# Self attention, element by element: each phase dequantises its own weights, and the search takes three steps a unit

## The chip, the cores and the metric

The kernel runs on one core of a Trainium2 chip. The metric is device time in microseconds (us) of one execution, the median of several runs. A profile is one further execution, recorded by the hardware profiler; its span runs from the first to the last instruction. A core has TensorE (PE) for matmuls with its weight loads (PEld), VectorE (DVE), ScalarE (ACT), GpSimd (POOL) and SyncE (SP), which here issues nearly all DMA transfers. Each engine takes its instructions in the order of the built program; semaphores make one engine wait for another.

## What is computed

One decoder layer over two batch elements of 512 tokens and 512 features, in float32: self attention, cross attention and a feed-forward part, each added to its input and normalised.

```python
q, k, v = (x @ (codes * repeat(scales, 32)) + b  for wq, wk, wv)   # 16 heads of 128
attn = softmax(q @ k.T / sqrt(128))
x = layernorm(x + (attn @ v) @ (wo_codes * repeat(wo_scales, 32)) + bo)
s = coef * (x @ Wq.T) @ ctx.T              # 1024 context rows
s = where(s < 54th largest of the row, -inf, s)
x = layernorm(x + softmax(s) @ ctx @ Wo.T)
x = layernorm(x + (silu(x @ Wg.T) * (x @ Wu.T)) @ Wd.T)
```

The weights of self attention come as codes and scales: a weight is a code times the scale of its block of 32 rows. This multiplication is called dequantising; it must be done on the chip before a weight is used.

## The kernel before

**Units, groups and phases.** The work of one head of one element is a unit. Four heads make a group; a group of one element is a phase of four units. There are 16 heads, so four groups and, for two elements, eight phases and 32 units. The list `phases` (L648) sets their order: group 0 of element 0, group 0 of element 1, then groups 1 to 3 of element 0, then groups 1 to 3 of element 1. `half_way` (L650) is the number of the first unit after element 0's last: 20. Phase 1 has no weights of its own: `owner` (L653) sends it to those of phase 0.

**A phase.** `values` (L719) computes v of four heads. For each unit, `queries_keys` (L736) computes q and k, `weights` (L771) the scores (PE, L785), the softmax (DVE and ACT) and its transpose: DVE turns blocks of 32 by 32 into the tile tq (L810), and 16 DMAs a unit move them into the tile pt (L818). `attend` (L824) multiplies pt with v (PE, L830) into the tile ot. When a phase is over, `project` (L859) multiplies its ot by wo and adds the result to the residual: DVE adds one part (L875) and POOL the other (L877), but for group 3, where DVE adds both (L874, L875).

**Strassen's products.** Most matmuls go through `seven` (L187 for the matmuls, L197 for the copies out of PSUM): a block product in seven instead of eight matmuls, in Winograd's form. It needs four sums of blocks of each operand. For the weights POOL makes them: tile wc for q and k (L107 to L110, four operations of 128x256), vc for v and oc for wo (four of 128x512 each). For ot, POOL makes otc (L116 to L119). Of the seven products, PE runs numbers 1, 2, 5, 6, 7 and 4, and 3 last; product 1 needs the first half of the dequantised weights, 2 and 4 the second, and 5, 6, 7 and 3 need sums.

**Weights.** Per unit, one DMA brings the codes wqk (0.5 MB) and one the scales sqk (0.5 MB). Per phase, wv and wo come with 1 MB of codes and two times 0.5 MB of scales (sv, so). POOL dequantises (L684) in halves: two operations of 128x512 a unit, and four each for wv and wo. The scales pass through three buffers (sc0 to sc2, L675) in turn, so a load of scales waits until the third one before it has been used. wv has one tile, and so has wo: a load waits until PE has read the last phase's.

**Order.** The loop (L961 on) runs over i, the unit that is attended to, with u = i + 2 the unit whose q, k and weights are computed. `due` tells at which u the scales are dequantised: those of unit u at u - 1, those of wv three and two units before a phase, those of wo three and four units after its start. The loads of scales are traced one unit earlier. A scheduler then reorders the instructions of each engine; the order on SP and POOL is fixed when the program is built.

**Start.** The first two units' weights and the first wv are dequantised on DVE, those of units 2 and 3 on POOL (L922 on). x transposed of element 1 (`load_xT(1)`) is loaded at the start and combined by POOL (`combine_x`) at i = 0. `load_residual` (at i = 0) brings x and adds the bias on POOL, in eight operations of 128x512.

**Cross attention of element 0** begins when element 0's self attention is over, amid the units of element 1. At i = half_way comes the layer norm, then its transpose, at half_way + 3 the queries (PE, L380), and at half_way + 3, 4, 5 and 7 the four score blocks (PE, L474). `clip` (L483) searches each block's 54th largest value on DVE, in steps of one MATCH_REPLACE8 (L493) and one MAX8 (L496); four blocks have 28 steps. `step` (L956) takes two before and two after the transposes of each unit from i = half_way + 4 on, and what is left is done at the last unit but one.

Of the kernel before, what the change touches and what calls it, by code (L numbers as in the profile page):

```python
# [24 lines left out]
def decoder_layer(  # L25
# [21 lines left out]
    nc = tc.nc  # L47
    B, S, D = x.shape
# [8 lines left out]
    GH = 4  # L57
    GW = GH * P
    NG = H // GH
# [173 lines left out]
    def load_xT(b):  # L233

        xt = place(f"xT{b}", (KD, S), f"x0T{b}")
        for n in range(2):
            nc.sync.dma_start(
                out=xt[:, n * HK : (n + 1) * HK, :],
                in_=xT[b, n * HD : (n + 1) * HD, :].rearrange("(k p) s -> p k s", p=P),
            )  # L240
        xts[b] = xt

    def combine_x(eng, b, name):
        xcs[b] = combine_b(eng, blocks(xts[b]), place(f"xc{b}", (4, HK, HS), f"{name}c{b}"))

    def load_residual():

        bo_sb = place("mt0", (D,), "bo_sb")
        nc.sync.dma_start(out=bo_sb, in_=bo.to_broadcast([P, D]))
        for b in range(B):  # L250
            rb[b] = place(f"res{b}", (NT, D), f"res{b}")
            nc.sync.dma_start(out=rb[b], in_=x[b].rearrange("(t p) d -> p t d", p=P))
            for t in range(NT):
                res[b, t] = rb[b][:, t, :]
                nc.gpsimd.tensor_tensor(res[b, t], res[b, t], bo_sb, ALU.add)
# [389 lines left out]

    phases = [(0, 0), (0, 1)] + [(g, b) for b in range(B) for g in range(1, NG)]  # L648
    units = [(g, b, j) for g, b in phases for j in range(GH)]
    half_way = (NG + 1) * GH  # L650
    last = len(phases) - 1

    def owner(p):  # L653
        return 0 if p == 1 else p

    def place_of_qk(u):

        return (u if u < GH else (u - GH) % 5) if u < half_way else (1, 2, 0)[(u - half_way) % 3]

    qkw, vw, ow, ks, qs, pts, vs, ots, raw = {}, {}, {}, {}, {}, {}, {}, {}, {}  # L660
    parts = {}
# [9 lines left out]
    def load_scales(key, n, queue):  # L671
        w, scales = raw[key]
        at, sv = scales[n]
        part = w if at is None else w[:, at, :]
        sct = place(f"sc{scale_count[0] % 3}", tuple(part.shape[1:]), f"s{key}_{n}")  # L675
        scale_count[0] += 1
        queue.dma_start(out=sct, in_=sv)
        parts[key, n] = (part, part, sct)

    def dequantise(eng, key, n=0):  # L680
        part, codes, sct = parts.pop((key, n))
        k = part.shape[1] // 2
        for w in (slice(0, k), slice(k, None)) if eng is nc.gpsimd else (slice(None),):
            eng.tensor_tensor(part[:, w], codes[:, w], sct[:, w], ALU.mult)  # L684

    def load_qk(u):
        g, b, j = units[u]
        h = g * GH + j
        load(f"qk{u}", f"wqk{place_of_qk(u)}", (KD, 2, P), wqk[h], [(None, wqk_s[h])])
# [11 lines left out]
    def load_o(p):  # L701
        g, b = phases[p]
        load(
            f"o{p}",
            "v0" if p == last else "wo",
            (GH, D),
            wo[g * GW : (g + 1) * GW, :].rearrange("(k p) f -> p k f", p=P),
            [(slice(n * 2, (n + 1) * 2), wo_s[g, n]) for n in range(2)],
        )

    def combine_qk(eng, u):
        w = raw[f"qk{owner(u // GH) * GH + u % GH}"][0]
        qkw[u] = combine_a(eng, blocks_pair(w), place(f"wc{u % 2}", (4, HK, P), f"wc{u}"))

    def combine_v(eng, p):
        w = raw[f"v{owner(p)}"][0]
        vw[p] = combine_a(eng, blocks_t(w), place("cmb0", (4, HK, GW // 2), f"vc{p}"))

    def values(p):  # L719
# [135 lines left out]
    def combine_o(eng, p):  # L855
        w = raw[f"o{p}"][0]
        ow[p] = combine_a(eng, blocks_t(w), place("wv" if p == last else "cmb1", (4, GH // 2, HD), f"oc{p}"))

    def project(p):  # L859

        g, b = phases[p]
        lo, hi = ots.pop((p, 0)), ots.pop((p, 1))
        oc = combine_b(
            nc.vector if p == last else nc.gpsimd,
            (lo[:, :, :HS], lo[:, :, HS:], hi[:, :, :HS], hi[:, :, HS:]),
            place("cmb0", (4, GH // 2, HS), f"otc{p}"),
        )
        rr = rb[b].rearrange("p (h s) (c f) -> p h s c f", h=2, c=2)
        for s in range(NT // 2):

            def add(z, u, s=s, c=1):
                o = rr[:, :, s, c, :]
                if g == NG - 1:
                    nc.vector.tensor_add(o, o, u)  # L874
                nc.vector.tensor_add(o, z, o)  # L875
                if g < NG - 1:
                    nc.gpsimd.tensor_tensor(o, o, u, ALU.add)  # L877

            seven(
                f"o{p}_{s}",  # L880
                oc,
                ow[owner(p)],
                slice(s * P, (s + 1) * P),
                add,
                lambda z, u, add=add: add(z, u, c=0),
            )
        close()
# [19 lines left out]
    for n in range(2):  # L907
        f = first[1][n]
# [21 lines left out]
    load_scales("qk2", 0, nc.sync)  # L930
    load_qk(3)
    load_scales("qk3", 0, nc.sync)
    load_xT(1)
    dequantise(nc.gpsimd, "qk2")
    combine_qk(nc.gpsimd, 2)
    dequantise(nc.gpsimd, "qk3")
    load_o(0)
    load_scales("o0", 0, nc.sync)
    load_scales("o0", 1, nc.sync)
    dequantise(nc.gpsimd, "o0", 0)  # L940
    dequantise(nc.gpsimd, "o0", 1)
    combine_o(nc.gpsimd, 0)


    due = {}
    for p in range(2, len(phases)):
        for j in range(GH):
            due.setdefault(p * GH + j - 1, []).append((f"qk{p * GH + j}", 0))
        for n in range(2):
            due.setdefault(p * GH - 3 + n, []).append((f"v{p}", n))  # L950
            due.setdefault((p * GH + 3 if p < last else p * GH + 2) + n, []).append((f"o{p}", n))

    XS = [half_way + n for n in (3, 4, 5, 7)]
    search0 = clips(0, ("work",))
# [1 line left out]
    def step(n):  # L956
        for _ in range(n):
            next(search0, None)

    lag = 2  # L960
    for i in range(len(units)):  # L961
        g, b, j = units[i]
        u = i + lag
        if u < len(units):
            gu, bu, ju = units[u]
            if ju == 0:
                values(u // GH)
            queries_keys(u)
            for key, n in due.get(u, []):
                dequantise(nc.gpsimd, key, n)  # L970
                if key == f"qk{u + 1}":
                    combine_qk(nc.gpsimd, u + 1)
                    if ju == GH - 1:
                        combine_v(nc.gpsimd, (u + 1) // GH)
                if key[0] == "o" and n == 1:
                    combine_o(nc.gpsimd, int(key[1:]))
            if u + 1 < 2 * GH:
                combine_qk(nc.gpsimd, u + 1)
                if u + 1 == GH:
                    combine_v(nc.gpsimd, 1)  # L980
        p = i // GH
        if j == 0 and 0 < p < last:
            project(p - 1)
            if p > 1:
                load_o(p)
        if i == len(units) - 2:
            project(last - 1)
            load_xw("wo", xwo, "wo")
        attend(i)
        if i > half_way + 3:  # L990
            step(2)
        if u < len(units):
            weights(u)
            if i == last * GH - 1:
                load_o(last)
            if 2 * GH <= u + 3 < len(units):
                load_qk(u + 3)
            if ju == 0 and 1 < u // GH + 1 < len(phases):
                load_v(u // GH + 1)
            for key, n in due.get(u + 1, []):  # L1000
                load_scales(key, n, nc.sync)
        if i == 0:
            load_residual()
            combine_x(nc.gpsimd, 1, "x0")
        if i == 2 * GH:
            load_memT(0)
        if i == half_way:
            load_xw("wq", xwq, "cmb1")
            normal = normalise(0, "a")
            next(normal)  # L1010
        if i == half_way + 1:
            for _ in normal:
                pass
            turn_x(0, "xc0", "xT0", "x1T")
        if i == half_way + 3:
            xquery(0)
            score_tiles(0, (("wqk3", 1), ("wqk4", 1), ("xT0", 2)))
        if i in XS:
            xscores(0, XS.index(i))
        if i == XS[-1] + 1:  # L1020
            load_mem(0)
        if i > half_way + 3:
            step(2)
        if i == len(units) - 2:
            for _ in search0:
                pass
            free_sc = [f"sc{(scale_count[0] + n) % 3}" for n in range(3)]
            for _ in combine_mem(0, ("wqk2", *free_sc[:2])):
                pass
            transpose_weights(0, ("xT1", "xc1"))  # L1030
# [279 lines left out]
```

## Time and profile before

| | us |
|---|---|
| median of 3 runs | 1083.48 (1083.36 to 1083.54) |
| span of the profiled execution | 1082.2 |
| median less span | 1.3 |
| PE / PEld busy | 1070.7 / 796.8 |
| DVE / ACT / POOL busy | 611.0 / 408.6 / 575.6 |
| POOL: wqk dequantised (L684, 52 operations) | 66.2, 1.289 each |
| DMA moved | 142.71 MB |

A row of a timeline gives start, length, engine, line, operation, output tile and inputs, shape and count, and in brackets the idle time ahead of it and what ended that. A matmul of float32 appears as two records. A busy time is that of one engine; "idle before" is the time in which the engine did nothing ahead of such instructions. A stretch's row gives its length and the busy time and number of instructions of each engine, the granted TensorE clock, the share of the DMA engines and the GB/s.

### The profile page before, as it was taken

The page shows a single profiled execution, that of the slowest core. Times are in us where ns is not written, and L with a number is a line of the kernel's source. Part 1 is how long each engine was busy: PE and PEld are TensorE (multiplying, and loading weights), DVE is VectorE, ACT ScalarE, POOL GpSimd, SP SyncE. Part 2 cuts the span into 40 slices and gives each one's busy share as a digit, 9 for nine tenths or more (in the row PEclk, how much of TensorE's full clock was granted, in tenths as well). Part 3 has the DMA queues.
Part 4 walks back from the last instruction along what each step waited for, and adds up shares of the span by engine and source line. Part 5 has one row for each costly group of instructions (what it writes and reads, how often), then busy time and mean ns, then how long its engine had stood idle before and what let it go on. Part 6 is the DMA issues. An engine that isn't in the chain of part 4 may idle for free.

```text
span 1082.2 us, 12794 instructions
## 1 busy us (share of the span) xinstructions
PE 1070.7 (99%) x4252; PEld 796.8 (74%) x4252; DVE 611.0 (56%) x1015; ACT 408.6 (38%) x882; POOL 575.6 (53%) x578
## 2 busy tenths in 40 slices
PE   9999999999999999999999999999999999999997
PEld 5676776677677677665666567778888888888886
DVE  5444345335434445643898774468999736554254
ACT  3444435335344533733444353222443214221221
POOL 4955546846945856514952654525565812264530
PEclk9999999999999999999999999999999999999999
DMA  9535446545553555536332537331214401422201
GB/s 350 156 105 176 157 134 220 181 142 161 198 191 95 173 172 156 194 81 182 136 117 78 139 115 253 89 106 39 97 65 132 137 20 51 163 86 76 94 19 39
DMA packets 66257, 142.71 MB, mean 132 GB/s; under 512 B 12560, under 2 KB 12560, under 8 KB 66192
## 3 DMA queue, kind: packets, MB, share of 16 engines
q1 hardware_dynamic: 65472, 140.32, 41.4%
q10 hardware_dynamic: 720, 1.57, 0.4%
q8 instruction: 34, 0.56, 0.2%
q14 instruction: 31, 0.25, 0.1%
HBM read 99.90 MB, written 2.10 MB: 94 GB/s over the span
## 4 chain that ended last, share of the span: by engine, by line
PE 82%; DVE 13%; ACT 3%; DMA 1%; POOL 1%; issue 1%; DVEq 0%; ACTq 0%; POOLq 0%
PE sc L785 10%; PE av L830 9%; PE zqk L187 9%; PE zgu L187 7%; PE rqk L187 7%; PE rgu L187 5%; PE zo L187 5%; PE zv L187 5%; PE zpd L187 4%; PE ro L187 4%; DVE work L493 4%; DVE top L496 3%; PE rv L187 3%; PE rpd L187 3%; PE zxav L187 3%; PE xs L474 2%
## 5 line engine op out<-in xcount | busy, mean ns | idle before, releaser
L830 PE MATMUL av<-pt,v 128*128 128x512 f32 x256 | 121.8, 592 | 0.0
L796 DVE TENSOR_REDUCE nm<-sc 128x2 f32<-128x1024 f32 x63 | 76.9, 1222 | 78.9 <-PE sc L785 78.9
L785 PE MATMUL sc<-k,q 128*128 128x512 f32 x256 | 117.2, 599 | 0.0
L799 ACT ACTIVATE p<-sc,nm 128x512 f32<-128x512 f32 x128 | 86.8, 681 | 75.8 <-DVE nm L796 75.8
L810 DVE STREAM_TRANSPOSE tq<-p 128x512 f32<-128x512 f32 x128 | 84.9, 699 | 38.0 <-ACT p L807 36.2
L785 PEld LDWEIGHTS sc<-k,q 128*128 128x128 f32 x256 | 47.2, 190 | 62.4 <-issue 50.6
L807 ACT ACTIVATE p<-p,sm 128x512 f32<-128x512 f32 x128 | 85.4, 715 | 1.5 <-DVE sm L806 1.3
L107 POOL TENSOR_TENSOR wc<-wgu 128x256 f32<-128x256 f32 x32 | 24.9, 779 | 111.9 <-PE zgu L187 69.3
L684 POOL TENSOR_TENSOR wqk<-wqk,sqk 128x512 f32<-128x512 f32 x52 | 66.2, 1289 | 32.5 <-DMA wqk<-in_wqk 22.4
L197 ACT ACTIVATE ugu<-rgu 128x256 f32<-128x256 f32 x96 | 36.2, 378 | 103.0 <-PE rgu L187 100.8
L830 PEld LDWEIGHTS av<-pt,v 128*128 128x128 f32 x256 | 48.6, 190 | 30.5 <-issue 26.8
L187 PE MATMUL rgu<-x2c,wc 128*128 128x256 f32 x256 | 66.2, 381 | 1.0 <-ACT ugu L197 1.0
L187 PE MATMUL rqk<-x0c,wc 128*128 128x256 f32 x248 | 65.0, 384 | 0.3 <-ACT uqk L197 0.2
L496 DVE MAX8 top<-work 128x8 f32<-128x1024 f32 x48 | 58.6, 1221 | 0.9
L848 ACT ACTIVATE ot<-av,bqkv_sb 128x512 f32<-128x512 f32 x28 | 19.2, 687 | 101.4 <-PE av L830 101.4
L187 PEld LDWEIGHTS rgu<-x2c,wc 128*128 128x128 f32 x256 | 48.2, 190 | 8.9 <-ACT ugu L197 1.9
L187 PEld LDWEIGHTS rqk<-x0c,wc 128*128 128x128 f32 x248 | 45.1, 189 | 12.2 <-ACT uqk L197 5.1
L1134 DVE TENSOR_TENSOR gt<-zgu,ugu 128x512 f32<-128x512 f32 x32 | 21.9, 684 | 48.9 <-PE zgu L187 48.9
L107 POOL TENSOR_TENSOR wc<-wqk 128x256 f32<-128x256 f32 x31 | 22.6, 730 | 49.8 <-PE zqk L187 49.7
L493 DVE MATCH_REPLACE8 work<-top,work 128x1024 f32<-128x1024 f32 x40 | 48.3, 1208 | 0.0
L877 POOL TENSOR_TENSOR res<-res,uo 128x512 f32<-128x512 f32 x24 | 30.7, 1280 | 29.8 <-DVE res L875 26.2
L116 POOL TENSOR_TENSOR otc<-ot 128x512 f32<-128x512 f32 x7 | 8.9, 1270 | 66.9 <-PE zv L187 66.9
(313 smaller groups left out, 2465.8 us busy)
## 6 DMA issues: line engine op xcount, KB each, us to landing
pt<-tq SPq DMA_DIRECT2D x512, 64.0 KB, 2.0
wgu<-in_wgu SPq DMA_DIRECT2D x32, 512.0 KB, 3.2
wqk<-in_wqk SPq DMA_DIRECT2D x26, 512.0 KB, 5.5
sqk<-in_wqk_s SPq DMA_DIRECT2D x26, 512.0 KB, 4.1
wdn<-in_wdn SPq DMA_DIRECT2D x8, 1024.0 KB, 5.7
sv<-in_wv_s SPq DMA_DIRECT2D x14, 512.0 KB, 5.8
wv<-in_wv SPq DMA_DIRECT2D x7, 1024.0 KB, 5.2
wo<-in_wo SPq DMA_DIRECT2D x7, 1024.0 KB, 5.6
```

The source lines that it names most:

```text
L107: eng.tensor_tensor(c[0], a10, a11, ALU.add)
L187: nc.tensor.matmul(o, left[k][:, cols], right[k], start=start and k == 0, stop=k == len(left) - 1, skip_group_check=not start,)
L197: nc.scalar.activation(u[:, i, :], r, AF.Identity, bias=at, scale=scale)
L493: nc.vector.match_replace(work, top, src, LOWEST)
L496: nc.vector.max(top, work)
L684: eng.tensor_tensor(part[:, w], codes[:, w], sct[:, w], ALU.mult)
L785: nc.tensor.matmul(pair[n], q[:, (t + n) * P : (t + n + 1) * P], k, start=True, stop=True,)
L796: nc.vector.reduce_max(nms, scs, axis=AX.X, negate=True)
L799: nc.scalar.activation(pr, pair[t % 2], AF.Exp, bias=nms[:, t % 2 : t % 2 + 1], accum_out=sm,)
L807: nc.scalar.activation(pr, pr, AF.Copy, scale=sm)
L810: nc.vector.transpose(tq[:, :, :, t, :].rearrange("p n k c -> p k n c"), pr.rearrange("p (k n a) -> p k n a", n=NB, a=BLK),)
L830: nc.tensor.matmul(av, vs[u // GH][:, k, j * P : (j + 1) * P], pt[:, :, k, :], start=(k == 0), stop=(k == NT - 1),)
```

## The change

The phases run element by element: groups 0 to 3 of element 0, then groups 1, 2, 3 and 0 of element 1. `half_way` is 16. `owner` is gone: each phase loads, dequantises and combines its own weights, so phase 1 does so too. The entries of `due` are made for all phases, with the scales of phase 1's wv at u = 2 at the earliest. Element 1's x is loaded and combined at i = 10. wo of phase 0 is dequantised through `due` and not ahead of the loop. Of the search, one step is taken before and two after each unit's transposes. The last projection is now that of group 0, so POOL makes its second addition.

```diff
-    phases = [(0, 0), (0, 1)] + [(g, b) for b in range(B) for g in range(1, NG)]
+    phases = [(g, 0) for g in range(NG)] + [((g + 1) % NG, 1) for g in range(NG)]
     units = [(g, b, j) for g, b in phases for j in range(GH)]
-    half_way = (NG + 1) * GH
+    half_way = NG * GH
...
-    def owner(p):
-        return 0 if p == 1 else p
...
-        return (u if u < GH else (u - GH) % 5) if u < half_way else (1, 2, 0)[(u - half_way) % 3]
+        return u % 5 if u < half_way else (1, 2, 0)[(u - half_way) % 3]
...
-        w = raw[f"qk{owner(u // GH) * GH + u % GH}"][0]
+        w = raw[f"qk{u}"][0]
...
-        w = raw[f"v{owner(p)}"][0]
+        w = raw[f"v{p}"][0]
...
-                ow[owner(p)],
+                ow[p],
...
-    load_xT(1)
     dequantise(nc.gpsimd, "qk2")
     combine_qk(nc.gpsimd, 2)
     dequantise(nc.gpsimd, "qk3")
+    load_v(1)
     load_o(0)
-    load_scales("o0", 0, nc.sync)
-    load_scales("o0", 1, nc.sync)
-    dequantise(nc.gpsimd, "o0", 0)
-    dequantise(nc.gpsimd, "o0", 1)
-    combine_o(nc.gpsimd, 0)
+    load_qk(GH)
...
     due = {}
-    for p in range(2, len(phases)):
-        for j in range(GH):
+    for p in range(len(phases)):
+        for n in range(2):
+            if p:
+                due.setdefault(max(p * GH - 3 + n, 2), []).append((f"v{p}", n))
+            due.setdefault((p * GH + 3 if p < last else p * GH + 2) + n, []).append((f"o{p}", n))
+        for j in range(GH if p else 0):
             due.setdefault(p * GH + j - 1, []).append((f"qk{p * GH + j}", 0))
-        for n in range(2):
-            due.setdefault(p * GH - 3 + n, []).append((f"v{p}", n))
-            due.setdefault((p * GH + 3 if p < last else p * GH + 2) + n, []).append((f"o{p}", n))
+    for key, n in due[2]:
+        load_scales(key, n, nc.sync)
...
-            if u + 1 < 2 * GH:
+            if u + 1 < GH:
                 combine_qk(nc.gpsimd, u + 1)
-                if u + 1 == GH:
-                    combine_v(nc.gpsimd, 1)
...
             project(p - 1)
-            if p > 1:
-                load_o(p)
+            load_o(p)
...
         if i > half_way + 3:
-            step(2)
+            step(1)
...
-            if 2 * GH <= u + 3 < len(units):
+            if GH < u + 3 < len(units):
                 load_qk(u + 3)
-            if ju == 0 and 1 < u // GH + 1 < len(phases):
+            if ju == 0 and u // GH + 1 < len(phases):
                 load_v(u // GH + 1)
...
         if i == 0:
             load_residual()
+        if i == half_way - 6:
+            load_xT(1)
             combine_x(nc.gpsimd, 1, "x0")
```

## The prediction, made before the changed kernel had run

> **What bounds the kernel now.** I read the page first, its busy times.
>
> ```profile
> PE 1070.7 (99%) x4252; PEld 796.8 (74%) x4252; DVE 611.0 (56%) x1015; ACT 408.6 (38%) x882; POOL 575.6 (53%) x578
> ...
> PEclk9999999999999999999999999999999999999999
> ```
>
> TensorE (PE) is the bound: 1070.7 of 1082.2 us, at full clock. The two programs, listed engine by engine, hold the same instructions on PE, DVE and ACT (2144, 961 and 761 rows' worth); POOL gets 20 more and SP 14 more DMAs. So the change can only move PE's idle time, and that needs a view by stretches: us, PE busy, PEld, DVE, ACT, POOL, clock, DMA share, GB/s.
>
> ```profile
> 27.00:54.00 27.00, 27.00 (x100) 18.29 (x99) 12.94 (x21) 11.74 (x28) 26.45 (x25) 1.00 0.53 157
> ...
> 432.00:459.00 27.00, 26.25 (x92) 16.87 (x91) 18.09 (x34) 19.53 (x40) 15.12 (x14) 1.00 0.63 206
> ...
> 567.00:594.00 27.00, 26.74 (x104) 19.02 (x103) 24.47 (x40) 11.89 (x25) 9.10 (x9) 1.00 0.27 78
> ```
>
> The reader is to see three things: after the first stretch PE idles at most 0.75 us in 27 until the attention ends; POOL has stretches near full (26.45) that PE does not feel; the search (40 DVE instructions, 24.47 us of DVE) costs PE 0.26 us.
>
> Third, the timelines of SP, POOL and PE, for how far ahead the weights come. SP first: 16 "pt" moves of one unit (one head of one element) hold SP for 10 us, and what stands behind them waits.
>
> ```profile
> 28.44 10.35 SPq L818 DMA_DIRECT2D pt<-tq  x16
> ...
> 45.29 24.28 SPq L818 DMA_DIRECT2D pt<-tq  x32
> ...
> 75.80 10.01 SPq L818 DMA_DIRECT2D pt<-tq  x16
> ...
> 285.62 0.33 SPq L677 DMA_DIRECT2D sqk<-in_wqk_s  x1
> ```
>
> Then POOL and PE.
>
> ```profile
> 265.62 2.49 POOL L684 TENSOR_TENSOR wqk<-wqk,sqk 128x512 f32<-128x512 f32 x2 [5.45 <-DMA sqk<-in_wqk_s]
> ...
> 283.10 2.50 POOL L684 TENSOR_TENSOR wo<-wo,so 128x512 f32<-128x512 f32 x2
> ...
> 56.57 4.96 POOL L255 TENSOR_TENSOR res<-res,bo_sb 128x512 f32<-128x512 f32 x4
> ```
> ```profile
> 77.98 1.03 PE L187 MATMUL zqk<-x0T,wqk 128*128 128x256 f32 x4
> ...
> 87.46 3.60 PE L785 MATMUL sc<-k,q 128*128 128x512 f32 x8
> 90.89 1.03 PE L187 MATMUL rqk<-x0T,wqk 128*128 128x256 f32 x4
> ...
> 321.39 1.03 PE L187 MATMUL rqk<-x0T,wqk 128*128 128x256 f32 x4
> ```
>
> The scales of unit 17 are issued at 285.62, dequantised on POOL by 295.8 and combined by 301.1; PE takes them at 321.39. That is 20 us of cover, about a unit and a half (a phase of four units is 77 us long: 87.46 to 164.3 between like scores). The listing says why: before, the scales of unit u stand on SP four to five units of "pt" ahead (sqk17 behind pt13, sqk20 behind pt15). After, they stand behind pt of u-2 (units 4 to 7, 13, 15, 16, 17, 19, 21 to 23) or u-3: two units, some 26 us of PE time at 12.9 us a unit, are gone. Phase 1 used to run on the weights already dequantised for phase 0, and that pause let loads run ahead. It is what the change removes.
>
> **The change, part by part.**
>
> Removed early: load of the second element's x, its four combinations on POOL (5 us), and the early wo scales. They only move to unit 10; no gain, since PE has no idle time there.
>
> Added on POOL: 8 of wqk at 1.27, and 12 of wv, wo, oc at 1.25: 25 us. On a queue 53% busy they cost nothing by their sum; they cost where PE waits. Added DMAs: 8 MB of 143, also nothing by sum.
>
> *Durations.* POOL: 1.24 a 128x512 operation in a row, 1.35 if it reads the one before; 0.70 and 0.80 for 128x256. A unit's weights need 2 halves (2.5) and 4 sums (3.0). PE: 0.86 for each of a unit's seven products; 1 needs the first half, 2 the second, 5 the second sum, 6 the third, 3 the fourth. Landing after issue: 3.3 us for a lone 0.5 MB of scales (262.17 to 265.62), 6.0 behind 1 MB (86.48 to the wv row at 92.53); each 0.5 MB ahead 1.3. "pt" of a unit starts 10 us after its scores start and ends 20.7 after.
>
> *Unit 4.* pt2 ends at 69.6 as before; behind it SP issues so0 (lands 73.3), sqk4 (74.6). POOL, idle since 54.7, does wo half (75.9), one sum (77.2), wqk4 (78.4 and 79.7), sums (80.4, 81.1, 81.9, 82.7). PE is there at 78.0 (order after matches the row at 77.98) and starts product 6 at 82.1 instead of 80.6: **1.5 us**.
>
> *Unit 5.* POOL goes on: first residual 5.0 (87.7), an otc sum (88.9), second residual 5.0 (93.9), the other wo half (96.3), two sums (99.0), wqk5 halves around a sum (100.3, 102.8), sums with otc between (103.5, 104.2, 106.2, 108.1). PE comes at 90.89 + 3.4 (all of unit 3's values product now stands ahead) + 1.5 = 95.8. Product 1 starts 100.4, 2 at 102.9, 5 at 104.3, 6 at 106.3 instead of 98.4: **7.9 us**. The residual's 10 us on POOL stood in the same place before, but nothing behind them was late.
>
> *Unit 6.* Its scores come at 109.8, pt4 ends at 109; behind it wqk7, wv2 and sqk6: lands 116.8, halves to 119.4, sums to 121.7. PE comes at 116.7 and starts product 6 at 121.8 instead of 119.3: **2.5 us**. Unit 7 has a projection (12 us) ahead: nothing. First phase: 11.9 us.
>
> *Later units.* Same arithmetic from the start V of the scores of u-2. Unit 17: pt15 ends V+20.7; wqk18, so3, sqk17 land V+24.6, 25.9, 27.2; POOL: wo half 28.4, sums 31.1, wqk17 32.4 and 34.9 with a sum between, its sums 36.3, 37.1, 37.9. PE comes at V+32.8 and starts product 6 at 37.3 instead of 35.4: 1.9. Unit 18 follows it: three otc sums (41.8), halves 43.1 and 44.3, sums to 46.6; PE wants the first at 39.9, the third sum at 44.9 after that: 5.1. **7.0** together. Units 13 and 14, same without the three otc sums: **3.8**. Unit 16 (so3, sqk16 behind pt14; wo half and a sum first): third sum at 33.1 after unit 14's scores against a need at 30.2: **2.9**. Unit 10's projection: the otc sums stand behind wqk11 and wc11, 1.9 late or not at all: **1.0**. Units 15, 19, 21 have a finished values product or a projection ahead of them: nothing. From unit 22 the second element's half has the cross attention's matmuls (13.7 us of queries, 3.4 per score block) as cover: nothing. Later units: 14.7 us. If every scale lands at 3.3 instead, each term falls by up to 1.3; at 6.0 it rises as much; so 9 to 20 here and 10 to 14 in the first phase.
>
> *Gained.* Three steps of 2.4 us a unit instead of four, over twelve units instead of eight: PE's idle time from 540 to 648 is 0.92 us by the stretches, that at the switch (432:459) 0.75, gaps below a stretch's rounding 0.3: at most **2.0**, at least 0; I take 2.0, most of it being tied to DVE.
>
> *End of attention.* The last projection is now of group 0, so its four u-adds go from DVE (0.69 each) to POOL (1.27), ahead of the layer norm: about 1.4 us later. The transposed result lands at 706.0, PE takes it at 709.0: hidden by 3 us; uncovered it costs 1.4.
>
> Sum: 11.9 + 14.7 - 2.0 = 24.6. The profiled execution's span is 1082.2, and 1.3 lie around it to the median of 1083.48: 1082.2 + 24.6 + 1.3 = **1108.1**.
>
> A clock row to weigh: eight warming matmuls took 3.78 us (from 1.18), at 216 ns they would take 1.73, so a cold PE runs at half speed; after that no PE pause here reaches 1 us and the clock stays 1.00. The Trainium skill, "TensorE: Matmul & The Clock Gate", section "Part 1: The HAM clock gate", says that an idle window of about 3.4 us brings half clock back for about 3.4 us. That speaks against the change: unit 5's 4.5 us pause may do it; by the rule the sum would be about 1.7 us more, by the rows 0. I leave it out.
>
> **Rivals.**
>
> *Only the first phase (0.25).* POOL idles before each group of later scales; if those land or run a few us sooner than I put them, every later term is cut to zero while residual and late scales still meet at units 4 to 6. 1083.5 + 11.9 - 2.0 = 1093.4.
>
> *POOL bound all along (0.12).* Units 15, 19, 21, the projections and the layer norm's handover each lose the one or two us of cover that I give them, eight places at 1.5: 1108 + 12 = 1120.
>
> *Nothing is late (0.07), or a gain (0.06).* The mechanism: POOL's 25 us fit in its idle time, at unit 5 above all. It decides there: it needs wqk5's first half by 95.8, so wo's other half and one residual would have to be done by then; then only the search's relief counts: 1083.5 - 2.0 = 1081.5, or 1083.5 if the search's relief is nil. For it: POOL is 53% busy and 26.45 of 27 at the start without hurt. Against: SP's order puts the scales behind pt.
>
> **Numbers.** Likeliest 1108 (0.50; by its own bounds 1099 to 1116), 1093 (0.25), 1120 (0.12), 1083.5 (0.07), 1081 (0.06). Range 1090 to 1119: it leaves out the last two and half of the third. A measurement here tells 0.2% (2.2 us) from no change: faster 0.06, same 0.07, slower 0.87.
>
> **What would show it.** In the changed profile: PE idle between about 95 and 110 us, released by POOL (wc, wqk); POOL waiting for sqk and so, then working without pause from 73 to 109; idle again about the scores of units 13, 16 to 18; nothing between 440 and 650. Wrong if PE stays over 26.5 of 27 us from 81 to 135, if its pauses are released by pt or v, or if the loss sits after 650.

## The result, and the profile after

| | before | after |
|---|---|---|
| median, us | 1083.51 (4 runs) | 1119.14 (1118.11 to 1120.04, 4 runs) |
| ratio after/before | | 1.0324, 95% interval 1.0311 to 1.0337 |
| span of the profiled execution, us | 1082.2 | 1118.2 |
| POOL: wqk dequantised | 52 operations, 66.2 us | 60 operations, 75.1 us |

The change costs 36 us, 3.2%. It was predicted at 1108.1, with 1090 to 1119 as the range: the time came out at the very end of the range. First the page of after: busy times, the granted clock, and the rows of dequantising.

```profile
PE 1083.3 (97%) x4252; PEld 798.7 (71%) x4252; DVE 614.5 (55%) x1015; ACT 411.1 (37%) x882; POOL 599.2 (54%) x598
...
PEclk9998999999999999999999999999999999999999
...
L681 POOL TENSOR_TENSOR wqk<-wqk,sqk 128x512 f32<-128x512 f32 x60 | 75.1, 1270 | 58.0 <-DMA wqk<-in_wqk 20.0
```

PE still has 4252 records but is 97% busy instead of 99%, and 12.6 us busier (1083.3 against 1070.7) for the same work: part of it ran at a lower clock, which the 8 in the PEclk row marks. While PE worked, 13.65 us ran at half clock, so that makes at most 6.8 of the 12.6. Another part is that a pause counts as idle only after the modelled end of the last matmul: at unit 5's wait for k, below, the next start comes 1.55 us late and 1.38 of that is idle. The stretches say where the time went (us; PE, PEld, DVE, ACT and POOL busy; granted clock; DMA share; GB/s).

```profile
54.00:81.00 27.00, 25.78 (x97) 17.46 (x95) 11.90 (x21) 12.66 (x30) 7.60 (x8) 1.00 0.59 173
81.00:108.00 27.00, 21.04 (x62) 12.83 (x62) 7.58 (x13) 8.13 (x17) 26.17 (x25) 0.89 0.45 124
108.00:135.00 27.00, 24.82 (x96) 17.78 (x95) 8.97 (x15) 9.83 (x22) 10.76 (x11) 0.98 0.54 170
243.00:270.00 27.00, 24.12 (x81) 15.86 (x80) 8.96 (x15) 8.30 (x18) 14.48 (x14) 0.94 0.60 199
351.00:378.00 27.00, 24.02 (x94) 18.17 (x95) 10.09 (x17) 9.04 (x21) 12.75 (x13) 0.94 0.35 93
432.00:459.00 27.00, 23.91 (x67) 12.43 (x68) 8.94 (x16) 10.74 (x23) 8.24 (x9) 1.00 0.59 178
567.00:594.00 27.00, 27.00 (x109) 20.16 (x108) 24.13 (x35) 10.44 (x21) 20.79 (x20) 1.00 0.69 210
675.00:702.00 27.00, 25.93 (x118) 18.82 (x117) 13.82 (x17) 9.53 (x19) 8.00 (x6) 1.00 0.73 238
```

From 81 to 108 us PE is busy 21.04 us where it was busy 27.00, while POOL works 26.17 of 27. The other holes are units 13 (243 to 270), 17 and 18 (324 to 378, of which the second stretch is shown) and 21 (432 to 459). The search (567 to 594) is full. Who ended PE's idle time is in the waits (us in total, times, longest):

```profile
PE rqk L187 <- POOL wqk L681: 10.5, 6, 4.3
PE zqk L187 <- POOL wqk L681: 4.0, 3, 1.3
PE zqk L187 <- DVE k L744: 3.3, 4, 1.4
PE sc L782 <- DVE q L745: 1.6, 2, 0.8
```

In the kernel before, POOL stood nowhere in this list, and its longest entry was 1.2 us at the start. The two kinds of pause, and a third loss between them, are all in unit 5's rows on PE:

```profile
100.96 1.13 PE L187 MATMUL rqk<-x0T,wqk 128*128 128x256 f32 x4 [4.33 <-POOL wqk L681]
103.40 2.07 PE L187 MATMUL zqk<-x0T,wqk 128*128 128x256 f32 x4 [1.31 <-POOL wqk L681]
105.27 1.91 PE L187 MATMUL zqk<-x0c,wc 128*128 128x256 f32 x4
106.97 1.91 PE L187 MATMUL rqk<-x0c,wc 128*128 128x256 f32 x4
...
112.03 1.10 PE L187 MATMUL zqk<-x0T,wc 128*128 128x256 f32 x4 [1.38 <-DVE k L744]
113.92 3.70 PE L782 MATMUL sc<-k,q 128*128 128x512 f32 x8 [0.79 <-DVE q L745]
```

PE waits 4.33 and 1.31 us for the halves of wqk; then products that take 1.03 us elsewhere take 1.9 to 2.1, at half clock; then it waits 1.38 us for k and 0.79 for q, with no other work between product 4 (here the four records at 109.62) and product 3, nor between product 3 and the scores. POOL's timeline shows what kept wqk5 (the rows at 99.64 and 102.09) waiting:

```profile
82.92 4.94 POOL L255 TENSOR_TENSOR res<-res,bo_sb 128x512 f32<-128x512 f32 x4
87.82 1.26 POOL L116 TENSOR_TENSOR otc<-ot 128x512 f32<-128x512 f32 x1
89.05 4.93 POOL L255 TENSOR_TENSOR res<-res,bo_sb 128x512 f32<-128x512 f32 x4
94.49 2.51 POOL L681 TENSOR_TENSOR wo<-wo,so 128x512 f32<-128x512 f32 x2 [0.52 <-DMA so<-in_wo_s]
97.08 1.26 POOL L107 TENSOR_TENSOR oc<-wo 128x512 f32<-128x512 f32 x1
98.42 1.27 POOL L108 TENSOR_TENSOR oc<-oc,wo 128x512 f32<-128x512 f32 x1
99.64 1.26 POOL L681 TENSOR_TENSOR wqk<-wqk,sqk 128x512 f32<-128x512 f32 x1
100.86 1.26 POOL L110 TENSOR_TENSOR oc<-wo,oc 128x512 f32<-128x512 f32 x1
102.09 1.26 POOL L681 TENSOR_TENSOR wqk<-wqk,sqk 128x512 f32<-128x512 f32 x1
...
118.37 2.50 POOL L681 TENSOR_TENSOR wqk<-wqk,sqk 128x512 f32<-128x512 f32 x2 [8.63 <-DMA sqk<-in_wqk_s]
```

Residual, otc and wo stand ahead of wqk5; wqk6 waits 8.63 us for its scales.

**PE's lost time by cause.** Over the whole trace, for each two neighbouring matmul records, take the time between their starts less the commonest spacing of the first one's shape (0.108, 0.216 and 0.429 us for 128, 256 and 512 columns), and put the excess to the second one's releaser. The line "half clock" is the excess behind records that start while the granted clock is half, where neither POOL nor k or q is the releaser. Some experiments stand beside, for later; each column is one execution, and that of e1 was its fastest (1119.5 us).

| lost, us | before | after | e1 | e5 | e7 | e8 | e11 | e12 |
|---|---|---|---|---|---|---|---|---|
| POOL's weights and otc | 0 | 19.9 | 23.2 | 17.5 | 7.4 | 0.7 | 4.5 | 11.1 |
| half clock | 0 | 5.7 | 2.4 | 8.3 | 4.2 | 0 | 0 | 3.0 |
| k and q (DVE) | 2.5 | 7.3 | 7.0 | 9.1 | 7.5 | 7.0 | 8.0 | 7.1 |
| all else | 18.8 | 24.2 | 24.3 | 29.1 | 29.3 | 27.3 | 27.7 | 29.3 |
| sum | 21.3 | 57.1 | 56.9 | 64.0 | 48.4 | 34.9 | 40.3 | 50.5 |

The sums differ by 35.8 us from before to after, the spans by 36.0. So 25.6 us of the loss are late weights with the clock they cost, 4.8 are k and q, and 5.4 are spread over small waits.

### The profile page after: what moved, and what is told of

Same layout as the page of the kernel before. It is cut to its first block, busy times and chain, and to the rows that moved or that the text cites. A ratio compares the mean times of both kernels' runs of the same rounds, so it can differ in the third digit from the quotient of the medians.

```text
span 1118.2 us, 12868 instructions
## 1 busy us (share of the span) xinstructions
PE 1083.3 (97%) x4252; PEld 798.7 (71%) x4252; DVE 614.5 (55%) x1015; ACT 411.1 (37%) x882; POOL 599.2 (54%) x598
## 4 chain that ended last, share of the span: by engine, by line
PE 68%; DVE 11%; POOL 7%; ACT 4%; SPq 3%; DMA 3%; issue 2%; DVEq 0%; ACTq 0%; POOLq 0%
PE sc L782 7%; PE zqk L187 7%; PE zgu L187 7%; PE av L827 6%; PE rgu L187 5%; PE rqk L187 5%; PE zo L187 5%; PE zpd L187 4%; PE ro L187 3%; PE rpd L187 3%; SPq L815 3%; DVE work L493 3%; PE zv L187 3%; PE zxav L187 2%; DVE top L496 2%
## 5 line engine op out<-in xcount | busy, mean ns | idle before, releaser
L681 POOL TENSOR_TENSOR wqk<-wqk,sqk 128x512 f32<-128x512 f32 x60 | 75.1, 1270 | 58.0 <-DMA wqk<-in_wqk 20.0
L681 POOL TENSOR_TENSOR wo<-wo,so 128x512 f32<-128x512 f32 x32 | 39.9, 1270 | 58.7 <-DMA so<-in_wo_s 49.2
L197 ACT ACTIVATE uqk<-rqk,bqkv_sb 128x256 f32<-128x256 f32 x62 | 29.3, 472 | 71.4 <-PE rqk L187 68.7
L874 POOL TENSOR_TENSOR res<-res,uo 128x512 f32<-128x512 f32 x24 | 30.3, 1267 | 43.2 <-DVE res L872 37.5
L681 POOL TENSOR_TENSOR wv<-wv,sv 128x512 f32<-128x512 f32 x28 | 36.4, 1308 | 25.4 <-DMA wv<-in_wv 22.1
```

The lines of the kernel that those rows point to most:

```text
L197: nc.scalar.activation(u[:, i, :], r, AF.Identity, bias=at, scale=scale)
```

## The experiments

The theory at the outset was the prediction's: scales issued late on SP make POOL late. Its rivals were that POOL's larger amount of work costs by itself, and that the order of the phases does. Ratios are to the kernel before, timed beside each; us are medians.

| run | edit, in a few words | us | ratio (95% interval) |
|---|---|---|---|
| e1 | scales ahead of pt | 1123.7 | 1.0354 (1.0335 to 1.0372) |
| e2 | residual later | 1124.4 | 1.0369 (1.0353 to 1.0384) |
| e3 | e1 and e2 | 1122.7 | 1.0338 (1.0313 to 1.0363) |
| e4 | old order, own weights | 1112.1 | 1.0259 (1.0244 to 1.0274) |
| e5 | otc and u-additions on DVE | 1125.3 | 1.0379 (1.0357 to 1.0400) |
| e7 | e5 with e1 | 1110.4 | 1.0243 (1.0228 to 1.0258) |
| e8 | wqk two units ahead | 1097.5 | 1.0127 (1.0112 to 1.0142) |
| e9 | two steps of the search | 1117.0 | 1.0315 (1.0289 to 1.0340) |
| e10 | element 1 ends in group 3 | 1117.5 | 1.0319 (1.0295 to 1.0342) |
| e11 | old order, wqk two units ahead | 1102.8 | 1.0168 (1.0151 to 1.0185) |
| e12 | e8, loads ahead of pt | 1113.8 | 1.0269 (1.0254 to 1.0284) |

### e1: the scales ahead of the pt moves

```diff
-            weights(u)
             if i == last * GH - 1:
                 load_o(last)
-            if GH < u + 3 < len(units):
-                load_qk(u + 3)
             if ju == 0 and u // GH + 1 < len(phases):
                 load_v(u // GH + 1)
             for key, n in due.get(u + 1, []):
                 load_scales(key, n, nc.sync)
+            weights(u)
+            if GH < u + 3 < len(units):
+                load_qk(u + 3)
```

> The changed kernel, with each unit's loads of scales (and those of wv's and the last wo's codes) traced ahead of the unit's 16 pt moves instead of behind them: about one unit of pt, 13 us, earlier on SP; POOL's work is the same. Late scales (my theory): POOL's waits for sqk and so shrink, and of the 36 us the 21 that the trace shows after the first phase (7.4 at units 13 and 14, 8.7 at 17 and 18, 3.9 at 21, the rest small) go, with 2 at unit 4 and part of unit 5's: 1085 to 1097 us. POOL's amount (rival: 25 us more work on POOL is what costs, wherever the scales stand): within 2 us of 1119. Order of the phases (rival: element by element costs by itself): within 2 us of 1119.

Measured 1123.7 us (1119.5 to 1123.9): no gain at all. My theory in that form is refuted. The trace shows why. In after, POOL's waits for the scales so came to 49.2 us and those for sqk to 16.4; in e1 neither is among its largest waits any more, but three others are longer (us in total, times, longest, in e1):

```profile
POOL otc L116 <- PE zv L187: 67.3, 5, 20.1
POOL otc L117 <- ACT ot L845: 48.1, 5, 11.4
POOL res L874 <- DVE res L872: 47.3, 12, 6.8
```

(In after the first and third are 36.2 and 37.5, and the second is not in the list.) These are waits for the attention's own results, and POOL takes its instructions in order. Unit 6 on POOL's timeline of e1:

```profile
110.68 1.26 POOL L117 TENSOR_TENSOR otc<-ot,otc 128x512 f32<-128x512 f32 x1 [9.07 <-ACT ot L845]
111.90 1.26 POOL L118 TENSOR_TENSOR otc<-ot,ot 128x512 f32<-128x512 f32 x1
113.12 1.26 POOL L119 TENSOR_TENSOR otc<-ot,otc 128x512 f32<-128x512 f32 x1
114.35 2.48 POOL L681 TENSOR_TENSOR wqk<-wqk,sqk 128x512 f32<-128x512 f32 x2
```

The scales of wqk6 were issued at 92.16 and their row has no wait of its own; yet POOL sits idle for 9.07 us, because otc stands ahead of it in the queue and waits for ACT's copy of ot. So there are two gates in a row, SP's queue and POOL's, and opening the first only hands the wait to the second. That is the new theory: POOL dequantises only just ahead of use, and what costs is the loss of its lead, not one late transfer. (An edit on one queue also moves the built order of others: in e1, 504 of PE's 4252 records stand in other places than in after. So a run's time is read with its waits beside it.)

### e2 and e3: the residual moved away from unit 5

```diff
-    def load_residual():
+    def load_residual(bs):
...
-        for b in range(B):
+        for b in bs:
...
-        if i == 0:
-            load_residual()
+        if i == 2:
+            load_residual([0])
+        if i == 6:
+            load_residual([1])
```

> The changed kernel, with the residual's loads and its eight additions of bo on POOL moved from unit 0 to units 2 (element 0) and 6 (element 1), away from unit 5's weights. Late scales, with the residual in the way at unit 5 (my theory): wqk5 is ready about 10 us sooner, so unit 5's two pauses of 4.5 and 1.5 us go, with them the half-speed matmuls behind them (about 3.4 us) and the 2.5 us at its k and q: 1105 to 1112 us, and no row of half clock about 102 to 109 us; the later losses stay, at units 13, 17, 18 and 21. POOL's amount or the order of the phases (rivals): the ten us only move, 1117 to 1121 us.

> The changed kernel with both edits: scales ahead of the pt moves, residual's additions at units 2 and 6. Late scales: PE waits for POOL nowhere for more than 1 us, the clock stays full, 1081 to 1088 us; if the end of the attention keeps its 1.5 to 2 us, 1083 to 1088. POOL's amount or order of the phases (rivals): above 1107 us.

Both missed: 1124.4 and 1122.7 us. In e2 the first pauses shrink (PE is idle 5.9 us from 54 to 135 instead of 9.4; unit 5's 4.33 us are gone, and unit 6 pauses for 2.66), but from 162 to 216 it is idle 6.0 us where in after it is 0.1. That is not the residual in a new place, for its additions stand at 119.84 and at 214.07, outside that stretch. It is the first gate again: POOL dequantises wo there at 160.94 and 177.31, after waits of 10.84 and 4.39 us for so, and the next wqk follows close behind each, at 164.74 and 182.45. SP issues these two loads of so at 155.99 and 172.81, each behind the pt of another unit; in after they went out at 139.07 and 147.82. In e3 PE is idle 1.6 us from 81 to 189 instead of 8.2, so both edits together do clear the first phase. Then PE waits 4.73 us for vc at 219.79, which POOL makes behind the second element's residual, and 6.11 us for wqk14 at 280.99, behind an otc that waits 17.33 us for ACT's ot.

### e4: the weights alone, in the old order

```diff
-    phases = [(g, 0) for g in range(NG)] + [((g + 1) % NG, 1) for g in range(NG)]
+    phases = [(0, 0), (0, 1)] + [(g, b) for b in range(B) for g in range(1, NG)]
-    half_way = NG * GH
+    half_way = (NG + 1) * GH
```

with element 1's x at the start and two steps of the search again, as in the kernel before.

> The weights part of the change alone: the phases in the order of the kernel before (group 0 of both elements, then 1 to 3 of the first, 1 to 3 of the second), two steps and two steps of the search, element 1's x at the start, but phase 1 loads, dequantises and combines its own weights. POOL's and SP's extra work and the places of the scales behind the pt moves are then those of the changed kernel. Late scales: the first phase's 13.7 us and units 13 to 18 stay as they are, 1108 to 1121 us. Order of the phases (rival): the loss goes, 1083 to 1087 us. POOL's amount (rival): 1112 to 1121 us.

Measured 1112.1, 27.7 us above the kernel before, timed beside it. So giving phase 1 weights of its own brings most of the loss without the new order; the rival that blames the order is refuted for that part. PE's pauses for wqk stand at units 5, 13, 17 and 21 again (4.20; 0.76 and 1.33; 1.16 and 1.34; 2.02 and 1.33 us), though not at unit 18.

### e5, e6 and e7: the waiting work taken off POOL

```diff
         oc = combine_b(
-            nc.vector if p == last else nc.gpsimd,
+            nc.vector,
...
-                if g == NG - 1:
-                    nc.vector.tensor_add(o, o, u)
+                nc.vector.tensor_add(o, o, u)
                 nc.vector.tensor_add(o, z, o)
-                if g < NG - 1:
-                    nc.gpsimd.tensor_tensor(o, o, u, ALU.add)
```

> The changed kernel, with the projections' work that waits for PE, ACT and DVE taken off POOL: the sums of ot (otc) and the additions of u run on DVE in every phase. The scales stay behind the pt moves. The runs before it have refuted late scales alone: with the scales ahead of pt the POOL's waits for DMA went, and its waits for the attention's results ahead of otc and res (before wqk, in the same queue) took their place. New theory, two gates in a row: POOL dequantises a unit's weights only just ahead of their use, and they stand behind late scales on SP and behind otc and res on POOL; either gate alone keeps the loss. Then this run, which opens one gate, gains only the otc sums between unit 5's, 18's and 21's weights: 1104 to 1118 us. Late scales alone: the same. POOL's amount (rival; POOL loses about 70 us of work here, three times what the change added): 1083 to 1090 us.

> The same kernel once more, for the spread of one look: the time of the run before within 0.5%.

e6 holds e5's kernel once more, though its label names the scales too: one run, 1127.6 us, 0.2% from e5's median. e7 is e5 with the edit of e1:

> The changed kernel with both gates opened: otc and the additions of u on DVE in every phase, and the scales traced ahead of the pt moves. Two gates in a row (my theory): POOL has neither late scales nor the attention's results ahead of wqk; the waits for POOL fall from about 20 us to under 8, less the 6 us that the run with DVE alone lost to DVE: 1090 to 1106 us. If it is neither gate (rival: the place of the weights in the built order of TensorE, with k and q uncovered, costs by itself): above 1112 us, with PE's waits for POOL small and its waits for DVE and ACT large.

e5 came to 1125.3 us, above its expected range, though POOL now does 54.6 us less than in after, by its page:

```profile
PE 1085.1 (96%) x4252; PEld 799.7 (71%) x4252; DVE 657.4 (58%) x1067; ACT 410.5 (36%) x882; POOL 544.6 (48%) x546
```

Its waits for scales (us in total, times, longest) are the reason:

```profile
POOL wo L681 <- DMA so<-in_wo_s: 88.0, 7, 26.2
...
POOL wqk L681 <- DMA sqk<-in_wqk_s: 44.6, 5, 13.8
```

The rival "POOL's amount" is refuted: twice the 25 us that the change added are gone, and PE's losses to POOL fall only from 19.9 to 17.5 us. (e8, below, shows it from the other side.) With gate two open, the first gate holds: POOL's waits for scales rise from 65.6 to 132.6 us. DVE does 43 us more, and "all else" is 4.9 us higher; that the one makes the other is likely, not shown. e7, with both open, came to 1110.4 us, above the 1106 I had allowed: the losses to POOL fall from 19.9 to 7.4 us, but "all else" stays at 29.3. Opening either gate alone leaves most of the loss to POOL or adds to it (23.2 in e1, 17.5 in e5); both together give back 12.5 us of it, and "all else" takes 5.1 of that.

### e8: the same work, one unit earlier

```diff
-            due.setdefault(p * GH + j - 1, []).append((f"qk{p * GH + j}", 0))
+            due.setdefault(max(p * GH + j - 2, 2), []).append((f"qk{p * GH + j}", 0))
...
-                if key == f"qk{u + 1}":
-                    combine_qk(nc.gpsimd, u + 1)
-                    if ju == GH - 1:
-                        combine_v(nc.gpsimd, (u + 1) // GH)
...
-            if u + 1 < GH:
+            if u + 1 < len(units):
                 combine_qk(nc.gpsimd, u + 1)
+                if ju == GH - 1:
+                    combine_v(nc.gpsimd, (u + 1) // GH)
```

> The changed kernel, with each unit's scales loaded and its wqk dequantised one unit earlier (at u-2 instead of u-1), the sums wc where they were. POOL's work is the same; on POOL, wqk5 and wc5 stand ahead of the residual and of the first otc, wqk9, 13 and 17 ahead of most of their phase's wo and oc. Two gates in a row: both leads grow by about a unit, so the waits for POOL fall by half or more: 1095 to 1110 us. Neither gate: 1116 to 1124 us.

Measured 1097.5 us: 22 of the 36 us are back, with no work taken away. The page of e8:

```profile
PE 1073.3 (98%) x4252; PEld 795.9 (73%) x4252; DVE 615.3 (56%) x1015; ACT 409.5 (37%) x882; POOL 601.0 (55%) x598
...
PEclk9999999999999999999999999999999999999999
```

POOL is as busy as in after (601.0 against 599.2), and PE's clock is full throughout. On POOL's timeline the place in the queue that held wqk4 now holds wqk5:

```profile
78.95 2.50 POOL L681 TENSOR_TENSOR wqk<-wqk,sqk 128x512 f32<-128x512 f32 x2
...
85.61 9.85 POOL L255 TENSOR_TENSOR res<-res,bo_sb 128x512 f32<-128x512 f32 x8
...
103.32 1.27 POOL L681 TENSOR_TENSOR wqk<-wqk,sqk 128x512 f32<-128x512 f32 x1
```

wqk5 is whole at 81.45 instead of 103.35, ahead of the residual's 9.85 us and not behind it, and the row at 103.32 is wqk6's second half. POOL still waits 52.5 us for so and 41.5 for DVE's res, but PE hardly does any more: by the table above its losses to POOL's weights come to 0.7 us. The largest of its waits in the attention are now

```profile
PE zqk L187 <- DVE k L744: 4.3, 4, 1.4
PE zo L187 <- ACT p L796: 1.4, 2, 0.7
PE zo L187 <- DVE res L872: 1.3, 2, 0.8
```

So the lead is the cause of the first 22 us: with POOL's work the same, the losses to POOL fall by 19.2 us and half clock by 5.7, while "all else" rises by 3.1. What is left, 13.6 us by the table of lost time, is not POOL but for the 0.7.

### e9 and e10: the search and the last projection

e9 has `step(2)` ahead of the transposes again, e10 `[(g, 1) for g in range(NG)]` for element 1's phases.

> The changed kernel with two steps of the search ahead of each unit's transposes, as before, instead of one. My prediction gave the relief 2.0 us: then 1121 us. The trace of the changed kernel shows no relief (PE loses 2.7 us there in both kernels): then within 1.5 us of 1119.

> The changed kernel with element 1's groups in the order 0, 1, 2, 3, so that the last projection is again of group 3 and DVE makes both of its additions. My prediction had the additions on POOL hidden: then within 1 us of 1119. The stretches from 648 to 702 us, 1.5 to 2 us worse than before, speak for the other case: 1117 to 1118 us.

1117.0 (1116.3 to 1121.6) and 1117.5 (1116.7 to 1122.6): both ranges overlap that of after. e9 turns out to be no experiment. In its trace the instructions of PE, PEld, DVE, ACT, POOL and SP stand in the same order as in after, by operation, tile and shape, all 1015 of DVE among them. As far as the trace tells, the scheduler sets the places of the search's steps, whatever `step` asks for. So the time of e9 is that of after's program once more, and the 2.1 us between them is how far two such timings lie apart. The part of the change that concerns the search never reached the engine either: in before, after and e9 alike the MATCH_REPLACE8 of element 0 come in bursts of 6, 12 and 6, over 115, 113 and 113 us. For e10 the 1.7 us to after lie within that spread. Its trace lacks one pause of after, 0.42 us for DVE's res at the last projection (718.68), and keeps the larger ones ahead of it.

### e11 and e12: what is left

e11 is e4 with the edit of e8. e12 is e8 with `weights(u)` moved behind all its loads, codes and scales.

> Phases in the order of the kernel before, each with its own weights, and wqk dequantised two units ahead. Lead (my theory): own weights cost only because they take POOL's lead away; with the lead given back, what is left is k and q without cover at units 5 and 13 in the built order of TensorE, 2.5 us each: 1087 to 1092 us, PE waiting for POOL's weights less than 1.5 us. Own weights cost by themselves (rival): the 13.6 us left by two units ahead in the new order stay, 1096 to 1100 us.

> The changed kernel with wqk dequantised two units ahead and, besides, the loads of codes and scales traced ahead of the pt moves, so that both queues lead by one unit more. In the built order of TensorE k and q are then without cover at unit 21 alone, instead of 13 and 17. Uncovered k and q as the largest part of what two units ahead left (my theory): 2 to 5 us less than that kernel, 1092 to 1096 us. POOL's queue again (rival: with the scales early, POOL waits for the attention at otc and res ahead of wqk): 1097 to 1106 us.

Both missed, and both by the second gate. e11: 1102.8 us. The lead gives back 9.4 of e4's 27.7 us, and PE's waits for k and q at units 5 and 13 cost 2.5 us each, as expected. But its POOL queue has one otc ahead of wqk6 that waits 4.72 us for ACT's ot at 106.20, and PE loses 4.1 us there. So neither "own weights cost nothing once the lead is back" nor "they cost 13.6 us by themselves" is shown. The order of the phases is no steady cost: the new order is 7.9 us above the old one with the short lead (35.6 less 27.7), and 4.9 us below it with the long one (13.4 against 18.3, each over its own kernel before).

e12: 1113.8 us. The time lies above the range of the rival too, but the rival names the cause: loads further ahead on SP make it worse than e8 by 16 us, and POOL's waits for the attention are longer than in e1 and e3 (us in total, times, longest):

```profile
POOL otc L116 <- PE zv L187: 84.7, 7, 17.9
POOL otc L117 <- ACT ot L845: 83.3, 5, 23.0
```

At 82.02 POOL's first otc has waited 12.74 us for PE; residual and wo stand behind it, and wqk6 behind them; PE's built order now has the first matmul of unit 6's product 1 ahead of unit 5's product 2 (in e8 it follows unit 5's scores), so PE stops there for 7.6 us with unit 5's products ready behind it. Cover on one queue is lost on the next.

## Why the prediction was right and where it was wrong

The time came out near the range's upper end, in part by luck; the steps below, each measured as the shift between like score rows of before and after, tell which part.

- **What bounds the kernel, and the timeline from 73 to 109: right.** Unit 5's products 1, 2, 5 and 6 were put at 100.4, 102.9, 104.3 and 106.3, and started at 100.96, 103.40, 105.27 and 106.97. wqk6's scales were put at 116.8; POOL got them at 118.37.
- **First phase: 11.9 predicted, 13.7 measured.** Unit 4 2.1 (1.5); unit 5 11.2 (7.9), because half clock and the waits for k and q come on top of the two pauses; unit 6 about 0.4 (2.5), since unit 5's delay had given it cover.
- **Later units.** Unit 10: 0.4 (1.0). Units 13, 14 and 16 together: 7.4 (3.8 and 2.9), nearly all at unit 13. Units 17 and 18: 8.7 (7.0). Unit 21: about 4 (nothing), 1.4 of it wqk and 2.5 k and q. A finished values product ahead of it was not enough.
- **Search: 2.0 gained, predicted; at most 0.3 measured.** Counted start to start, PE loses 2.1 us from the search's first MATCH_REPLACE8 to its last in before (512 to 627) and 1.8 in after (468 to 582). The step that failed is the spreading over twelve units: the built order of DVE holds the same three bursts in both kernels (see e9).
- **End of attention: nothing predicted.** By unit 21's scores 34.3 of the 36.0 us have come; the other 1.7 come behind them, search and feed-forward included. The last projection itself has a pause of 0.42 us, and e10 does not settle the rest.
- **The clock: weighed and left out; 5.7 us.** The prediction went by rows without a pause of 1 us; the pause that it put at 4.5 us itself was enough.

The sum: 24.6 predicted, 36.0 measured. The missing 11.4 are the first phase 1.8, units 13 to 18 2.4, unit 21 4.1, the search's 2.0 that did not come and the 1.7 behind unit 21, less 0.6 at unit 10. Two numbers of the prediction do not come out of its own rows: its terms give 1100.5 to 1115.5 as the bounds of the likeliest case, not 1099 to 1116, and a block of cross-attention scores takes 6.9 us of PE (16 records of 0.43), not 3.4, which makes more cover and no loss.

The sizes came near partly by luck, by two errors against each other. All predicted losses were waits for POOL's weights, 26.6 us before the search's relief; those waits measured 19.9. What made up for it were three things that the sum did not have: half clock 5.7, k and q 4.8, and 5.4 of small waits.

**The mechanism was half right.** That POOL comes late at units 4 to 6, 13 and 17 to 18, and that it isn't POOL's amount, held (e4, e5, e8). But the step "SP issues the scales behind pt, so POOL is late" names only the first of two gates: with the scales ahead of pt, the time did not fall (e1). The prediction took POOL's queue as a list of durations; its waits for PE, ACT and DVE at otc and res stood in the trace of before, as this line of its waits,

```profile
POOL otc L116 <- PE zv L187: 66.9, 7, 14.3
```

and were harmless there, where PE waits for no weights of POOL. What fails is a missing term: what stands ahead of wqk in POOL's queue once the scales are early. It did not show in the time of after, where the scales are late; it showed in e1, e3 and e12.

Of the rivals, "POOL bound all along" had the time (1120) and not the reason: it put eight further places at 1.5 us each (units 15, 19, 21, the projections and the layer norm), and of these only unit 21 lost more than that.

**What stays open** is the 13.6 us of e8. 4.5 of it are k and q. At units 13 and 17 of e8, as at units 5 and 21 of after, no matmul of other work stands between product 4 and product 3 (2 or more in before); each of these four loses 1.5 us at k, and three of them 0.9 more at q. But e8 also loses 1.5 us at k at unit 23 (485.49), with three of attend's matmuls between, so that order is not the whole reason. The rest, 8.5 us, are many small waits, the largest in the list 1.1 us, most of them for ACT and DVE. Why the order was built so was not tried. No run beat the kernel before.

## What to carry to other kernels

How far ahead of its use an operand is ready is a resource like any other: here a phase that needed no weights of its own had let SP and POOL run ahead, and that was lost when the phase got such work, 25 us on POOL. Follow the operand through every queue that it stands in, and ask at each what is ahead of it and what that waits for; opening one gate shows nothing while the next is shut. Giving the operand an earlier place in the queue (e8) was worth 22 us, while taking 55 us of other work off the engine (e5) was worth nothing. And before an edit is timed, compare the built order of the engines: e9's edit had left it as it was.

## What the runs showed of the hardware

The clock of TensorE falls in fixed windows. Four windows of after in a row (us; then the busy times as above, and the clock):

```profile
98.58:101.99 3.41, 1.03 (x4) 0.68 (x4) 0.71 (x1) 0.78 (x2) 3.41 (x3) 1.00 0.16 38
101.99:105.41 3.42, 2.11 (x6) 1.65 (x6) 0.00 (x0) 0.47 (x1) 3.42 (x5) 0.50 0.48 112
105.41:108.82 3.41, 3.41 (x10) 2.65 (x9) 0.00 (x0) 0.00 (x0) 3.41 (x5) 0.50 0.30 68
108.82:112.23 3.41, 2.03 (x10) 1.48 (x9) 0.69 (x1) 0.95 (x2) 0.92 (x1) 1.00 0.52 109
```

Half clock (0.50) lasts 6.83 us here and 3.41 us at 265.83 and at 357.99. These starts lie 48.0 and 27.0 times 3.413 us apart, whatever the kernel did in between. The Trainium skill, "TensorE: Matmul & The Clock Gate", section "Part 1: The HAM clock gate", gives a free-running window of 3413 ns, and that agrees. It also has the clock fall after at least one idle window, and here less was enough: no window of after was idle throughout (the idlest for 2.76 us), no pause but the first was as long as a window, and a pause of 2.77 us (before 357.34) and two close together of 1.56 and 1.32 us (before 262.94 and 265.39) brought half clock. Laid over the profiles of after and the twelve runs, from 30 to 1070 us, of the windows at full clock in which PE was idle for 2.0 us or more all 20 were followed by half clock; of those with 1.64 to 1.95 us idle, 11 of 20; of those with less, none. Of the windows at half clock, the 31 with at most 0.56 us idle were followed by full clock and the 14 with 0.65 us or more by half clock again, which fits the first stretch here, two windows long with 1.31 us idle in its first, and the others of one. The measurement decides: here some 60% of one window idle is enough, and whether a 2 us pause costs depends on where in the window it falls.
